# First rows of x ahead of the weights, constant rows behind the first store, a new table of rules

## The chip, the core and the metric

The kernel runs on one core of a Trainium2 chip. The metric is the device time of one execution in microseconds (us), as the median of several runs. Five engines work side by side, each through its own instruction stream in order: TensorE (PE, with its weight loads shown as PEld), VectorE (DVE), ScalarE (ACT), GpSimd (POOL) and SyncE (SP). In this kernel SP issues all the DMAs; "SPq" in a profile is the queue from which it does so.

## What is computed

Eight sequences of 1024 tokens with 256 channels go through one layer of four residual blocks, each behind a layer norm: a retention with its own norm, four heads and a gate; a feed-forward block with a shift by one token; an attention of 16 heads with a bias by relative position; and the same feed-forward block again.

```python
x = L0_attn_a_x                                   # (8, 1024, 256)
x = x + _L0_attn_a_ref(_layernorm(x), ln_w, ln_b, Wq, Wk, Wv, Wg, g_norm_w, Wo)
x = x + _L0_ffn_ref(_layernorm(x), W_r, W_k, W_v, mu_r, mu_k)
x = x + _L0_attn_b_ref(_layernorm(x), wq, bq, wk, bk, wv, bv, wo, bo, rel_bias)
x = x + _L0_ffn_ref(_layernorm(x), W_r, W_k, W_v, mu_r, mu_k)
```

Retention runs through a sequence in chunks with a state S per head: scores of a chunk, masked and decayed, times its values, plus the queries times S; then S is decayed and the chunk's keys times values are added. The attention is a softmax over all 1024 keys of scores plus a bias that depends on the distance of query and key alone, in 32 buckets.

## The kernel before

**A recorded program and a planner.** Nothing is issued while the functions of the kernel run. Each call on `act`, `dve`, `pool`, `sp` or `pe` is recorded as an operation (`Plan.record`) with an estimated cost, the operations it has to come after (`before`, found in `touch` from the parts of tiles that it reads and writes), and the target that `plan.target` had. `Plan.issue` then plays a clock of its own: at each step every free engine takes, among its operations whose inputs are done and whose tiles have a free buffer, the one with the lowest target, the older one of two equals. A DMA is taken to occupy SP for 0.4 us and to be done 2.0 us + bytes / 100 GB/s later, however many others are under way. The order so found is each engine's instruction stream. All instructions are issued from one line (L608, in `emit`), which is why groups in the profile are told apart by tiles.

**Rules and turns.** TensorE's choice has a correction. `RULES` holds sixteen rules: what a change of matmul mode costs, how many PSUM buffers must be free before scores are begun, how many sums to keep in hand, and four offsets by kind of matmul. `TURNS` holds one hexadecimal digit for each 20 us of the planned clock (`STRETCH`), which picks the rule of that time. It is a table of 122 digits.

**Stages.** For each sequence b: `retention(b)`, `ffn_front(b)`, `project_b(b)`, eight `maxima` and `shift` (attention scores p with queries as rows, for their maxima), four `weigh` (scores s with keys as rows, exponentials e, sums acc with the values va) and `back(b)` (output projection bop and the second feed-forward block). Their targets let the retention of the next sequence run beside the attention of this one.

**The head.** The first loads are `cm` (constants), `ln`, then `split(wqk, ...)`: two chunks of Wq and Wk into the tiles xo0 and xo1, cast by ScalarE into a rounded half wqk[0] and by VectorE's subtraction into the rest wqk[1]. `retention(0)` has the target -1.0 and loads its rows itself, in `prepare(c)`: a chunk of 256 tokens into xc, bn_stats on VectorE, the reciprocal roots on GpSimd (a_a, a_y, a_t, and at the end the product a_nb). `turn_chunk` makes z on ScalarE, transposes it on TensorE (ntp), evicts it twice on ScalarE and takes the difference on VectorE: nT, in two halves. Then come qps, vps and gps, the projections; ta and tb, the rotary products on VectorE; tps, qkT, aps, at, ops within the chunk and sps for the state S. In the first sequence `swift(b == 0)` sends to VectorE what GpSimd does later.

**later().** With the target -0.9 it is recorded after retention(0) and goes ahead of what of the retention has a later target: the other weights; hot, rel and ups for the bias (written to ud, read back as hk); bps for the bias of the output; and the constant rows of the stacked queries and keys. The DRAM tiles stk[0] (queries) and stk[1] (keys) hold 64 rows per head, in four blocks of 16: three blocks are written by `project_b` (qk, from TensorE's qkp), the fourth, from ROW_SHIFT on, holds constant rows. For the keys these depend on the head: VectorE multiplies stat by a factor fac, which comes from two small broadcast loads d31 and d0 ("d<-in_b_rel"), into kr, sixteen times, and each kr is stored twice. For the queries they are the same for all heads: two DMAs straight from c_stat in DRAM to stk[0] in DRAM, one for each of the two buffers (i = 0, 1; b % 2 picks one). Each repeats 16 rows of 1024 numbers for 16 heads:

```python
c_stat = ap["c_stat"]
for i in range(2):
    sp.dma_start(
        stk[0][i, ROW_SHIFT // AHD],
        bass.AP(tensor=c_stat.tensor, offset=c_stat.offset, ap=[[0, AH], [T, AHD], [1, T]]),
    )
```

**Who reads them.** `load_pair(b, j)` loads k and q of two heads from stk, all four blocks, for `maxima` and `weigh`. For b = 0 that comes after the four chunks of `project_b(0)`.

## Time and profile before

| | us |
|---|---|
| median of 3 runs (lowest to highest) | 2548.52 (2542.09 to 2551.93) |
| the profiled execution | 2557.27 |
| its span, from first to last instruction | 2555.5 |
| TensorE busy | 2476.2 (97%) |
| VectorE busy | 2107.5 (82%) |
| ScalarE busy | 2069.9 (81%) |
| GpSimd busy | 1589.0 (62%) |

The mean granted clock of TensorE is 0.992. The costliest groups on TensorE are acc (529.5 us), p (460.4) and s (456.7), all of the attention. The chain of work that ended last is TensorE for 79% of the span, VectorE for 8%, DMA for 5%, ScalarE for 3%.

In a timeline, a row has the start, the busy time, engine, line, operation, output<-input with shapes, the count of merged instructions, and in square brackets how long the engine had been idle before it and what it had waited for. A table by stage gives, for each stretch, its length, the busy time of each engine with its count of instructions, then TensorE's granted clock, the share of the DMA engines' time and GB/s.

### The profile page before, as it was taken

The numbers are of one execution on the slowest core, as the hardware profiler recorded it, in microseconds if no ns is written. First come the engines' busy times: TensorE is split into PE (matmuls) and PEld (weight loads), VectorE is DVE, ScalarE is ACT, GpSimd is POOL, SyncE is SP. The second block draws the span as 40 slices with busy tenths as digits, with TensorE's granted clock in tenths as the row PEclk, the third lists the DMA queues.
The fourth block names the chain that finished last, engine by engine and source line by source line (L and its number), as shares of the span: only waits on it lengthen the run. The fifth ranks groups of instructions, "written<-read, shape, count | busy, mean of one in ns | idle before, by whom it ended". The sixth has DMA issues, their size and how long they took to land.

```text
span 2555.5 us, 51508 instructions
## 1 busy us (share of the span) xinstructions
PE 2476.2 (97%) x15814; PEld 1459.8 (57%) x15814; DVE 2107.5 (82%) x6230; ACT 2069.9 (81%) x5334; POOL 1589.0 (62%) x2675
## 2 busy tenths in 40 slices
PE   5999999999999999999999999999999999999997
PEld 3887755555555555555555555555555555554555
DVE  6767998888888888988888788888888888788855
ACT  3565598888989888988888789988898888688883
POOL 2467666666756666666656576666666666666642
PEclk9999999999999999999999999999999999999999
DMA  7136322444344333332324333333233344444322
GB/s 175 42 108 150 81 58 68 130 107 112 85 106 105 84 100 101 110 98 79 92 64 119 97 107 102 94 78 109 68 94 93 102 118 115 124 115 113 93 64 72
DMA packets 252224, 251.17 MB, mean 98 GB/s; under 512 B 89042, under 2 KB 226180, under 8 KB 251924
## 3 DMA queue, kind: packets, MB, share of 16 engines
q1 hardware_dynamic: 251956, 247.89, 36.6%
q8 instruction: 132, 2.16, 0.4%
q14 instruction: 136, 1.11, 0.2%
HBM read 151.32 MB, written 98.59 MB: 98 GB/s over the span
## 4 chain that ended last, share of the span: by engine, by line
PE 79%; DVE 8%; DMA 5%; ACT 3%; POOL 2%; issue 1%; SPq 1%; POOLq 0%; DVEq 0%; ACTq 0%
PE acc L608 16%; PE p L608 10%; PE s L608 10%; PE kps L608 4%; PE wps L608 4%; PE yps L608 4%; PE rps L608 4%; PE qkp L608 3%; PE vps L608 3%; PE qps L608 3%; PE gps L608 3%; PE ops L608 3%; DVE pm L608 3%; ACT e L608 2%; PE bop L608 2%
## 5 line engine op out<-in xcount | busy, mean ns | idle before, releaser
L608 DVE TENSOR_REDUCE pm<-p 128x1 f32<-128x512 f32 (+2 forms) x2048 | 1057.2, 557 | 89.7 <-PE p L608 87.9
L608 ACT ACTIVATE e<-s 128x512 f32<-128x512 f32 (+2 forms) x2048 | 1008.0, 527 | 52.8 <-PE s L608 49.3
L608 POOL TENSOR_TENSOR e<-e,hk 128x512 f32<-128x512 f32 (+1 forms) x558 | 614.0, 1107 | 348.7 <-ACT e L608 326.9
L608 PE MATMUL acc<-e,va 128*17 128x512 f32 x4096 | 529.5, 599 | 3.7 <-ACT e L608 3.4
L608 DVE CUSTOM_DVE_ANT_0 jmax<-p,hk 128x256 bf16<-128x256 f32 (+1 forms) x1152 | 427.0, 371 | 111.8 <-PE p L608 106.6
L608 ACT COPY e<-s 128x256 f32<-128x256 f32 (+1 forms) x1116 | 400.0, 358 | 82.3 <-PE s L608 80.2
L608 PE MATMUL p<-k,q 64*128 64x512 f32 x2048 | 460.4, 438 | 5.0 <-DVE pm L608 2.8
L608 PE MATMUL s<-q,k 64*128 64x512 f32 x2048 | 456.7, 436 | 5.8 <-DVE pm L608 3.2
L608 ACT ACTIVATE e<-e 128x512 f32<-128x512 f32 (+1 forms) x576 | 336.2, 586 | 59.0 <-POOL e L608 56.1
L608 PEld LDWEIGHTS p<-k,q 64*128 64x128 f32 x2048 | 207.5, 185 | 248.4 <-ACT e L608 93.7
L608 PEld LDWEIGHTS s<-q,k 64*128 64x128 f32 x2048 | 206.0, 185 | 204.6 <-issue 69.8
L608 PEld LDWEIGHTS acc<-e,va 128*17 128x17 f32 x4096 | 77.7, 95 | 189.5 <-issue 161.6
L608 PE MATMUL kps<-xk,W_k 128*128 128x256 f32 x512 | 130.8, 399 | 10.7 <-DVE xk L608 9.7
L608 PE MATMUL rps<-W_r,xr 128*128 128x256 f32 x512 | 126.8, 390 | 3.0 <-DVE pm L608 1.8
L608 PE MATMUL yps<-W_v,xk 128*128 128x256 f32 x512 | 127.2, 392 | 1.1 <-DVE pm L608 0.5
L608 PE MATMUL wps<-wo_a,gs 128*128 128x256 f32 x512 | 125.7, 388 | 0.6 <-ACT gs L608 0.5
L608 PEld LDWEIGHTS kps<-xk,W_k 128*128 128x128 f32 x512 | 95.2, 195 | 40.7 <-issue 19.3
L608 PE MATMUL qps<-wqk,nT 128*128 128x512 f32 x384 | 106.8, 413 | 7.0 <-DVE nT L608 6.6
L608 PEld LDWEIGHTS rps<-W_r,xr 128*128 128x128 f32 x512 | 93.4, 191 | 34.5 <-DVE pm L608 5.1
L608 PEld LDWEIGHTS yps<-W_v,xk 128*128 128x128 f32 x512 | 93.6, 192 | 28.7 <-issue 12.0
L608 PEld LDWEIGHTS wps<-wo_a,gs 128*128 128x128 f32 x512 | 92.5, 190 | 26.5 <-issue 4.7
L608 POOL TENSOR_TENSOR ao_y<-ao_a,mhalf 128x4 f32<-128x4 f32 x64 | 65.7, 1026 | 66.5 <-DVE ao_a L608 65.8
(185 smaller groups left out, 4175.3 us busy)
## 6 DMA issues: line engine op xcount, KB each, us to landing
stk<-qk SPq DMA_DIRECT2D x192, 256.0 KB
hk<-ud SPq DMA_DIRECT2D x128, 256.0 KB
q<-stk SPq DMA_DIRECT2D x128, 256.0 KB
k<-stk SPq DMA_DIRECT2D x128, 256.0 KB
od<-o SPq DMA_DIRECT2D x64, 256.0 KB
vd<-vst SPq DMA_DIRECT2D x64, 136.0 KB
va<-vd SPq DMA_DIRECT2D x32, 272.0 KB
xc<-in_x SPq DMA_DIRECT2D x32, 256.0 KB
```

Of the source, the lines that this page charges most:

```text
L608: getattr(real, method)(*[be(a) for a in args], **{k: be(a) for k, a in kw.items()})
```

## The change

It has three parts. The load of the first 256 rows of x is recorded at the top, between `ln` and the split of Wq and Wk, with the target -1.1 of the first loads; `prepare(0)` of the first sequence takes that tile and issues no load. The two loads of the queries' constant rows leave `later()` for a function `constant_rows()`, called once, between `project_b(0)` and the first `maxima`. There they get the target -0.6 and, in the planner, one more operation to come after: the first store of queries (`stored[0]`). The load of stat stays where it was. And TURNS is another table of the same length, whose first three digits are the same.

```diff
 TURNS = (
-    "00070270877472bf8931ef967bfe1d0522ff04383dfe37be3f1f7ef668e19e9c33271224f3e73df5"
-    "5663e6176b19fd77763fbb3cafd79ff9fb9bf84111"
+    "0002022d5122719e9e58f469e3ffb30b577ab1d479fd79649f0576fe7dd0a2e7f1f59d76f22b7b64"
+    "d9edfed755b4febfbed95f00c5b15b912e8bbda111"
 )
...
+    first = plan.tile([P, HALF], F32, "xc", "xc", 4)
+    sp.dma_start(
+        first.rearrange("p (n d) -> p n d", n=2), x[0][:CT, :].rearrange("(n p) d -> p n d", p=P)
+    )
     split(wqk, ("a_Wq", "a_Wk"))
...
-        c_stat = ap["c_stat"]
-        for i in range(2):
-            sp.dma_start(
-                stk[0][i, ROW_SHIFT // AHD],
-                bass.AP(tensor=c_stat.tensor, offset=c_stat.offset, ap=[[0, AH], [T, AHD], [1, T]]),
-            )
         stat = plan.tile([P, T], F32, "k", "stat", NJ)
-        sp.dma_start(stat[:NSTAT], c_stat[1])
+        sp.dma_start(stat[:NSTAT], ap["c_stat"][1])
...
+    stored = []
+
+    def constant_rows():
+
+        c_stat, start = ap["c_stat"], len(plan.ops)
+        plan.target = -0.6
+        for i in range(2):
+            sp.dma_start(
+                stk[0][i, ROW_SHIFT // AHD],
+                bass.AP(tensor=c_stat.tensor, offset=c_stat.offset, ap=[[0, AH], [T, AHD], [1, T]]),
+            )
+        for op in plan.ops[start:]:
+            op.before.add(stored[0])
...
-            t = tile2k("xc", 4).rearrange("p (n d) -> p n d", n=2)
-            sp.dma_start(t, rows_in(x[b], c))
+            t = (first if b == c == 0 else tile2k("xc", 4)).rearrange("p (n d) -> p n d", n=2)
+            if b or c:
+                sp.dma_start(t, rows_in(x[b], c))
...
-                    sp.dma_start(rows_of(s, b, t0, p), pt[i].bitcast(F32))
+                    stored.append(sp.dma_start(rows_of(s, b, t0, p), pt[i].bitcast(F32)).n)
...
         project_b(b)
+        if b == 0:
+            constant_rows()
         for j in range(NPAIR):
```

## The prediction

> **What bounds the kernel now.** I read the page's busy times first, then tables of busy time by stage, then the timeline of the first 60 us, and last the queue that issues the DMAs (SP) around the place where the constant rows are to go.

> ```profile
> PE 2476.2 (97%) x15814; PEld 1459.8 (57%) x15814; DVE 2107.5 (82%) x6230; ACT 2069.9 (81%) x5334; POOL 1589.0 (62%) x2675
> ```

> TensorE is busy 2476.2 of 2555.5 us, so 79.3 us are idle. Where they lie decides what a change of order can win. Tables by stage put 31.2 us of them before 60 us, 14.1 us after 2500 us, and 34 us in the 2440 us between. The fields that matter in the next lines are the stretch, PE's busy time (first), DVE's (third), and near the end the granted clock, the share of the DMA engines and GB/s.

> ```profile
> 0.00:20.40 20.40, 2.91 (x8) 1.08 (x8) 8.19 (x22) 6.97 (x11) 7.74 (x29) 1.00 0.87 280
> 20.40:26.49 6.09, 1.45 (x2) 0.12 (x2) 0.00 (x0) 3.91 (x8) 0.00 (x0) 1.00 0.81 245
> 26.49:51.43 24.94, 15.86 (x88) 12.06 (x89) 21.89 (x46) 8.15 (x19) 2.57 (x3) 0.94 0.76 139
> 60.00:100.00 40.00, 39.52 (x260) 32.77 (x259) 28.69 (x66) 23.59 (x53) 18.05 (x57) 1.00 0.02 8
> ```

> The first 26 us are bound by DMA (0.81 to 0.87 of the engines' time); VectorE does nothing at all for 6.09 us; then VectorE is the bound up to 51.43 (21.89 of 24.94 us); from 60 us on TensorE is. So what the head gains, the end gains: behind it stands a full TensorE. The timeline says why VectorE stood still:

> ```profile
> 3.60 0.43 SPq L608 DMA_DIRECT2D xc<-in_x  x1
> ...
> 9.33 0.75 DVE L608 BATCH_NORM_STATS2 a_st<-xc 128x6 f32<-128x256 f32 x2 [1.33 <-DMA xc<-in_x]
> ...
> 14.84 0.64 SPq L608 DMA_DIRECT2D stk<-in_c_stat  x1
> ...
> 16.83 0.51 SPq L608 DMA_DIRECT2D stk<-in_c_stat  x1
> ...
> 17.36 1.09 ACT L608 ACTIVATE z<-xc,a_nb,a_y 128x256 f32<-128x256 f32 x2
> ...
> 18.47 0.92 SPq L608 DMA_DIRECT2D d<-in_b_rel  x2
> ...
> 26.49 0.16 DVE L608 TENSOR_TENSOR d<-d,d 16x16 f32<-16x16 f32 x1 [6.09 <-DMA d<-in_b_rel]
> ...
> 29.59 0.67 DVE L608 TENSOR_TENSOR nT<-z,nT 128x512 fp32r<-128x512 f32 x1
> ...
> 30.31 2.93 PE L608 MATMUL qps<-wqk,nT 128*128 128x512 f32 x6 [6.56 <-DVE nT L608]
> ...
> 50.54 0.40 DVE L608 COPY S<-sps 128x256 f32<-128x256 f32 x1
> ...
> 51.43 1.23 PE L608 MATMUL ops<-S,qkT 64*128 64x128 f32 x8 [5.25 <-ACT S L608]
> ```

> Two small loads (d, 1 KB each) land 7.5 us after their issue because two loads of constant rows, 16 x 16 x 1024 x 4 bytes = 1 MB each, stand before them. VectorE keeps its order, so nT, whose input ScalarE had finished by 22.4, waits behind d, and the first projection waits for nT. Later TensorE waits 5.25 us for S, which stands in VectorE's queue behind the sixteen kr products. That the constant rows hold the queue up is also in SP's waits:

> ```profile
> SPq L608 <- DMA stk<-in_c_stat: 3.9, 2, 2.7
> ```

> **The change, part by part.**

> (1) *Constant rows out of the head.* SP loses two issues (0.64 + 0.51 us), so the second d load goes out at 18.93 - 1.15 = 17.8. How fast it then lands no row shows, so it is bounded: by the first pair of weights, 3.2 us (second half issued at 2.18, cast at 5.40), and by the load of bwk, 5.4 us (issued 22.41, used 27.79). That is 21.0 or 23.2 instead of 26.49: 5.5 or 3.3 us won, and not above 6.09, the whole wait. I take 5.5: of the some 3.0 MB moved between 15 and 26.5 us (264, 303 and 120 GB/s), 2.1 are the constant rows, so little is left ahead. VectorE's queue itself is at 20.4 then, so the wait falls to some 0.6 us; what is late next is ups, hot and bwk, which arrive on the same queue earlier too.

> (2) *First rows of x ahead of the weights.* The issue moves from 3.60 to the third place, 1.70, past four weight loads (512 KB). It should land about when the first weights now do, 5.4, against 9.33: 3.9 us. That is not what the end gains. Its statistics were through at 14.6 (nb, the last input of z, ends then), yet z ran at 17.36, since ScalarE was held in front of it by the two casts of wg_a (15.49 and 16.84, waiting for their DMA). If the new order leaves z behind them, nothing is won beyond (1). If z goes first, the first projection could start near 17.4 (x at 5.4, the 5.3 us from there to the end of the nb chain as now, ScalarE free of the casts of wv_a at 11.3, then z, transposes, evictions and nT, 6 us as now from 17.36). Even so VectorE is the bound up to 51.43: the resumption of TensorE moves by no more than the work that VectorE can pull into its 12.2 idle us before 20.4: nT 0.67, ta 0.69 + 0.75, tb 0.74, vs 0.69 = 3.5 us. Bounds 0 to 3.5 more; I take 3.5, since the idle time is three times that. The weights passed land 256 KB later, 0.9 us at 282 GB/s; hidden, because the casts (5.40 to 8.0) come long before the first projection; without that cover 0.9 us.

> (3) *Constant rows after the first store.* Both issues stand now on SP behind the first store of queries. No other engine queues behind that store's wait; on SP what follows is:

> ```profile
> 101.28 0.89 SPq L608 DMA_DIRECT2D stk<-qk  x2
> ...
> 106.12 1.45 SPq L608 DMA_DIRECT2D stk<-qk  x3
> 126.83 0.36 SPq L608 DMA_DIRECT2D xd<-xc  x1
> ...
> 194.07 5.61 SPq L608 DMA_DIRECT2D q<-stk  x7
> ```

> Their first reader is q at 194.07. They take up to 8.7 us of the DMA engines (issued 16.83, released SP at 25.5, then beside other loads), and those are at 0.13 between 110 and 120 us. What can suffer is the load of xc at 104.03, read at 112.7: if the rows got ahead of it, 104.03 + 3.2 + 8.7 = 115.9, 3.2 us late. They become due only when the store is through, some microseconds after 101.28, so I take 0, with 0 to +3.2; a gain is excluded, since nothing there waits for less traffic. [...]

> (4) *The table of rules.* Its first three digits are the same, so the first 60 planned us keep their rules; from then on TensorE's choices differ nearly everywhere. No row shows the new order. Estimate from the spread of the present one: TensorE's idle time in the 24 stretches of 100 us from 100 to 2500 has a mean of 1.4 us and a deviation of some 1.25, so a whole order deviates by 1.25 x the root of 24 = 6 us, and the difference of two by 9. I take 0, with -9 to +9.

> Sum: -5.5 - 3.5 + 0 + 0 = **-9.0 us**. The profiled execution took 2557.27 us (span 2555.5 and 1.8 around it), so it would be 2548.3; it lay above the runs shown (2542.09 to 2551.93). On their median: 2548.52 - 9.0 = **2539.5**. The terms' ends give 2548.5 - 18.6 = 2530 and 2548.5 + 8.9 = 2557.

> [...]

> **Rivals.** *A: as summed,* 2539.5, own range 2530 to 2549.

> *B: the new order also loses a stall.* The present one has one bad place:

> ```profile
> 2180.00:2200.00 20.00, 14.70 (x84) 8.13 (x82) 15.53 (x54) 12.07 (x32) 10.85 (x17) 0.97 0.82 194
> 2200.00:2220.00 20.00, 20.00 (x99) 11.63 (x100) 14.45 (x41) 12.17 (x32) 14.43 (x25) 0.86 0.34 101
> ```

> There `bop` waited 4.8 us for `ob`, whose loads stood behind loads of pairs at a DMA share of 0.82, and the clock lost 20 x 0.03 + 20 x 0.14 = 3.4 us more: 8.2 together. It hangs on which loads meet, so another order need not have it: 2539.5 - 8.2 = 2531. Against it: the same chance can place one elsewhere.

> *C: the head doesn't do what it says.* If d stays behind other loads (wg, bwq, stat and hot are still ahead) and z behind the casts, only the 3.3 us of (1) or less remain: about 2546.

> *D: slower.* The new rules bring more stalls of just that kind, loads of the back stage meeting those of the pairs; there are eight such stages and one shows it now. Three more cost 24.6 us against the 9 won: 2564. It makes the kernel slower by over 0.5% from the third on ((12.7 + 9) / 8.2 = 2.6). For it: the planner gives each DMA a fixed latency, so it can't see such a meeting. Against it: seven of eight are free of it now.

> **How the numbers follow.** A measurement of this kernel tells about 0.5% from no change, 12.7 us: faster means below 2535.8, slower above 2561.3. Chances: A 0.44, of which 0.16 lies below 2535.8; B 0.28; C 0.08; D 0.20, of which 0.19 lies above 2561.3. Faster 0.16 + 0.28 = 0.44; same 0.28 + 0.08 + 0.01 = 0.37; slower 0.19. The time is A's, 2539.5. The range runs from 2520, below B's 2531 by the spread of (4), to 2565, which takes in A, C and the nearer half of D; about 0.05 is left below it and 0.10 above.

> **What would show it.** (1) is right if no load from c_stat is issued before 100 us and VectorE's wait for d is under 1.5 us. (2) is right if x's statistics start near 5.4 and the first qps before 22; C if qps starts after 25. TensorE's work after S should resume near 42.4 (51.43 - 9.0); if it resumes at 46 or later, VectorE's kr products or their stores set the head, and (2) was worth nothing. (3) is wrong if VectorE waits for xc between 105 and 130 us. (4): TensorE's idle time between 60 and 2500 us, 34 now; near 25 shows B, above 55 with a clock under 0.95 in several stretches shows D. The prediction fails most likely by (4), whose size nothing here shows.

## The result, and the profile after

| | before | after |
|---|---|---|
| median (lowest to highest), 9 runs each | 2547.17 (2542.09 to 2551.93) | 2557.92 (2556.54 to 2562.86) |
| the profiled execution | 2557.27 | 2556.74 |
| TensorE idle, 0 to 60 us | 31.2 | 25.2 |
| TensorE idle, 100 to 2500 us | 34.1 | 44.1 |
| TensorE busy, whole span | 2476.2 | 2472.1 |

The ratio is 1.0035, with an interval from 1.0026 to 1.0044: 10.8 us slower by the medians, where 9 less were forecast. It is inside the half per cent that I had called "no change", but nine runs of each are enough to tell it from nothing. The two profiled executions do not show it: that of before lay 10 us above its median, that of after 1 us below. So the two profiles are compared place by place, and the size of the change is taken from the timed runs.

First the page's busy times, which hardly moved; "after" does the same work:

```profile
PE 2472.1 (97%) x15814; PEld 1455.5 (57%) x15814; DVE 2109.2 (83%) x6230; ACT 2068.7 (81%) x5334; POOL 1588.0 (62%) x2675
```

The table by stage of after, in the stretches shown of before (length, PE, PEld, DVE, ACT and POOL busy; then granted clock, DMA share, GB/s):

```profile
0.00:20.40 20.40, 2.91 (x8) 1.08 (x8) 7.62 (x28) 6.17 (x10) 7.11 (x29) 1.00 0.75 237
20.40:26.49 6.09, 3.13 (x7) 2.48 (x8) 4.90 (x10) 5.10 (x11) 0.00 (x0) 1.00 0.59 108
26.49:51.43 24.94, 20.22 (x110) 14.93 (x109) 22.72 (x46) 9.91 (x23) 6.70 (x13) 0.87 0.66 139
60.00:100.00 40.00, 39.54 (x267) 33.40 (x266) 27.02 (x62) 23.36 (x54) 15.40 (x46) 1.00 0.10 29
550.00:600.00 50.00, 44.72 (x291) 23.67 (x289) 38.90 (x120) 40.30 (x108) 30.54 (x50) 0.95 0.53 139
2180.00:2200.00 20.00, 19.22 (x107) 10.94 (x99) 17.16 (x52) 13.66 (x36) 12.36 (x21) 1.00 0.88 225
```

VectorE, which stood still from 20.40 to 26.49, is now busy for 4.90 of these 6.09 us, and TensorE has 20.22 instead of 15.86 us of work in the next stretch. The one bad stretch of before, 2180 to 2200, is better (19.22 for 14.70). But 550 to 600 is new: 5.3 us idle, although the DMA share is only 0.53.

The timeline of after's first 60 us, in the lines that answer to those of before:

```profile
1.71 0.43 SPq L608 DMA_DIRECT2D xc<-in_x  x1
5.79 0.43 DVE L608 BATCH_NORM_STATS2 a_st<-xc 128x6 f32<-128x256 f32 x1 [4.12 <-DMA xc<-in_x]
...
13.14 1.09 ACT L608 ACTIVATE z<-xc,a_nb,a_y 128x256 f32<-128x256 f32 x2 [2.24 <-POOL a_nb L608]
...
16.91 0.87 SPq L608 DMA_DIRECT2D d<-in_b_rel  x2
...
17.11 1.86 PE L608 MATMUL bps<-wo_b,bv 128*1 128x256 f32 x4 [17.11 <-DMA bv<-in_b_bv]
...
18.90 1.11 PE L608 MATMUL ntp<-cm,z 128*128 128x128 f32 x4
...
19.34 0.15 DVE L608 TENSOR_TENSOR d<-d,d 16x16 f32<-16x16 f32 x1
...
22.63 0.67 DVE L608 TENSOR_TENSOR nT<-z,nT 128x512 fp32r<-128x512 f32 x1
...
23.36 2.93 PE L608 MATMUL qps<-wqk,nT 128*128 128x512 f32 x6 [3.35 <-DVE nT L608]
...
44.31 0.79 PE L608 MATMUL ops<-S,qkT 64*128 64x128 f32 x8 [3.52 <-ACT S L608]
```

The head does what the change says. VectorE's wait for d (6.09 us) is gone: d starts at 19.34 instead of 26.49. The first projection starts at 23.36 (30.31 before) and the work behind S at 44.31 (51.43): 7 us earlier. And the constant rows leave where they were meant to, with 92 us to go to their first reader:

```profile
101.03 0.87 SPq L608 DMA_DIRECT2D stk<-qk  x2
101.95 1.27 SPq L608 DMA_DIRECT2D stk<-in_c_stat  x2
```

The 7 us are given back later. These are the rows of after's timeline behind the largest idle times of TensorE between 100 and 2500 us; in each of these four, a DMA was late for the engine that releases TensorE, or for TensorE itself:

```profile
595.85 0.55 DVE L608 RECIPROCAL sums<-sums 128x64 f32<-128x64 f32 x1 [5.29 <-DMA sums<-od]
...
597.17 0.79 PE L608 MATMUL s<-q,k 64*128 64x512 f32 x2 [4.55 <-DVE pm L608]
...
941.83 0.43 DVE L608 BATCH_NORM_STATS2 a_st<-xc 128x6 f32<-128x256 f32 x1 [4.40 <-DMA xc<-in_x]
...
943.08 0.47 PE L608 MATMUL s<-q,k 64*128 64x512 f32 x1 [1.81 <-DVE pm L608]
...
2262.28 1.26 POOL L608 TENSOR_TENSOR ob<-ob,os 128x512 f32<-128x512 f32 x1 [7.70 <-DMA ob<-od]
...
2263.59 3.68 PE L608 MATMUL bop<-wo_b,ob 128*128 128x256 f32 x8 [3.55 <-POOL ob L608]
...
2324.40 0.74 PE L608 MATMUL s<-q,k 64*128 64x512 f32 x2 [2.15 <-DMA q<-md]
```

The first pair of lines reads: VectorE had the reciprocal of the sums next in its order, and their load, issued at 593.64, released it 2.2 us later; the pm that would have freed a PSUM buffer stood behind it, and TensorE had nothing to do for 4.55 us. With a fifth one (p at 201.95, 2.43 us, for which the profile names no wait, and 0.39 for a load of k behind it) these stalls are 14.9 us. Before had one of this size:

```profile
2199.95 3.78 PE L608 MATMUL bop<-wo_b,ob 128*128 128x256 f32 x8 [4.79 <-POOL ob L608]
```

The difference is as large as the 10.0 us by which TensorE's idle time in the middle grew. That it fits so well is partly chance: waits of 1.0 to 1.6 us are 10.0 us in before (eight of them) and 3.8 us in after (three), and the waits under 1 us make up for that.

### The profile page after: what moved, and what is told of

Same layout as the page of the kernel before. It is cut to its first block, busy times and chain, and to the rows that moved or that the text cites. A ratio compares the mean times of both kernels' runs of the same rounds, so it can differ in the third digit from the quotient of the medians.

```text
span 2554.7 us, 51543 instructions
## 1 busy us (share of the span) xinstructions
PE 2472.1 (97%) x15814; PEld 1455.5 (57%) x15814; DVE 2109.2 (83%) x6230; ACT 2068.7 (81%) x5334; POOL 1588.0 (62%) x2675
## 3 DMA queue, kind: packets, MB, share of 16 engines
q8 instruction: 133, 2.18, 0.4%
## 4 chain that ended last, share of the span: by engine, by line
PE 77%; DVE 11%; DMA 5%; ACT 4%; POOL 2%; issue 1%; SPq 0%; POOLq 0%; DVEq 0%; ACTq 0%
PE acc L608 15%; PE p L608 10%; PE s L608 10%; PE kps L608 4%; PE wps L608 4%; DVE pm L608 4%; PE yps L608 4%; PE rps L608 4%; PE qkp L608 3%; PE qps L608 3%; PE ops L608 3%; PE gps L608 3%; PE vps L608 3%; ACT e L608 2%; DVE xr L608 2%; PE bvp L608 2%
## 5 line engine op out<-in xcount | busy, mean ns | idle before, releaser
L608 DVE TENSOR_REDUCE pm<-p 128x1 f32<-128x512 f32 (+2 forms) x2048 | 1057.3, 557 | 82.9 <-PE p L608 81.0
L608 ACT ACTIVATE e<-s 128x512 f32<-128x512 f32 (+2 forms) x2048 | 1006.6, 528 | 51.9 <-PE s L608 47.4
L608 POOL TENSOR_TENSOR e<-e,hk 128x512 f32<-128x512 f32 (+1 forms) x558 | 611.9, 1104 | 318.1 <-ACT e L608 304.1
L608 DVE CUSTOM_DVE_ANT_0 jmax<-p,hk 128x256 bf16<-128x256 f32 (+1 forms) x1152 | 427.9, 371 | 133.3 <-PE p L608 127.8
L608 PE MATMUL acc<-e,va 128*17 128x512 f32 x4096 | 526.6, 599 | 1.0 <-ACT e L608 0.6
L608 ACT COPY e<-s 128x256 f32<-128x256 f32 (+1 forms) x1116 | 400.1, 358 | 92.9 <-PE s L608 90.4
L608 PE MATMUL p<-k,q 64*128 64x512 f32 x2048 | 460.9, 438 | 6.5 <-DVE pm L608 2.5
L608 PE MATMUL s<-q,k 64*128 64x512 f32 x2048 | 452.2, 435 | 13.2 <-DVE pm L608 10.3
L608 ACT ACTIVATE e<-e 128x512 f32<-128x512 f32 (+1 forms) x576 | 335.3, 587 | 39.2 <-POOL e L608 36.1
L608 PEld LDWEIGHTS p<-k,q 64*128 64x128 f32 x2048 | 207.6, 185 | 243.1 <-ACT e L608 75.8
L608 PEld LDWEIGHTS s<-q,k 64*128 64x128 f32 x2048 | 203.3, 185 | 197.2 <-issue 73.0
L608 PEld LDWEIGHTS acc<-e,va 128*17 128x17 f32 x4096 | 79.0, 96 | 197.4 <-issue 168.9
L608 PE MATMUL rps<-W_r,xr 128*128 128x256 f32 x512 | 127.5, 391 | 8.7 <-DVE xr L608 5.2
L608 PE MATMUL kps<-xk,W_k 128*128 128x256 f32 x512 | 129.0, 395 | 4.8 <-DVE xk L608 3.8
L608 PE MATMUL yps<-W_v,xk 128*128 128x256 f32 x512 | 127.2, 392 | 1.0 <-POOL xk L608 0.6
L608 PE MATMUL wps<-wo_a,gs 128*128 128x256 f32 x512 | 125.5, 388 | 1.2 <-DVE pm L608 0.5
L608 POOL TENSOR_TENSOR ao_y<-ao_a,mhalf 128x4 f32<-128x4 f32 x64 | 66.0, 1031 | 81.9 <-DVE ao_a L608 81.1
L608 PEld LDWEIGHTS rps<-W_r,xr 128*128 128x128 f32 x512 | 93.0, 191 | 38.3 <-issue 6.2
L608 PEld LDWEIGHTS kps<-xk,W_k 128*128 128x128 f32 x512 | 94.3, 193 | 33.2 <-issue 12.3
L608 PE MATMUL qps<-wqk,nT 128*128 128x512 f32 x384 | 108.3, 418 | 3.9 <-DVE nT L608 3.3
L608 PEld LDWEIGHTS yps<-W_v,xk 128*128 128x128 f32 x512 | 93.8, 192 | 29.2 <-issue 11.8
L608 PE MATMUL vps<-wv_a,nT 128*128 128x512 f32 x384 | 106.0, 412 | 0.9 <-DVE pm L608 0.8
```

The lines of the kernel that those rows point to most:

```text
L608: getattr(real, method)(*[be(a) for a in args], **{k: be(a) for k, a in kw.items()})
```

## The experiments

**Each part with a table that was not found for it.** The first four kernels put the parts together anew: (e1) after with the old table, (e2) before with the new table, (e3) before with the load of x first, and (e4) before with the constant rows late. e1, e3 and e4 have the old table.

```diff
# e1: head of the change, old TURNS        # e2: old head, new TURNS
+    first = plan.tile([P, HALF], F32, "xc", "xc", 4)          # e1, e3
+    sp.dma_start(first.rearrange(...), x[0][:CT, :].rearrange(...))
...
+    def constant_rows():                                      # e1, e4
...
-    "00070270877472bf8931ef967bfe1d0522ff04383dfe37be3f1f7ef668e19e9c33271224f3e73df5"
+    "0002022d5122719e9e58f469e3ffb30b577ab1d479fd79649f0576fe7dd0a2e7f1f59d76f22b7b64"   # e2
```

> The change without its table: first rows ahead, constant rows late, the old digits. Head as in the changed kernel: first qps near 23.4 us, work after S resumed near 44.3, 7.1 us before the old kernel. Theory T (the new digits' order costs the 17 us that lie between the head's -7 and the +10.75 measured): 2547 - 7 = 2540. Theory R (the late constant rows cost it): 2557 as with the new digits. Theory L (every change of order is a draw, because DMAs land later than the planner thinks wherever they meet; the old kernel's draw was a good one): the head moves everything against the digits' stretches, so this is a new draw too, anywhere in 2535 to 2562, with other stalls at other places than either kernel, each behind a late DMA.

> The old kernel with the new digits alone: head as before (qps near 30.3, resumed near 51.4). Theory T: 2547 + 17 = 2564. Theory R: 2547, the digits cost nothing. Theory L: a new draw with the head's 7 us not won, 2542 to 2569, with stalls at places that are not those of the changed kernel, so that the two parts do not add.

> The old kernel with the first rows ahead of the weights alone; constant rows early, old digits. By my sum the head gains little here: VectorE still waits for d behind the constant rows, so first qps 28 to 30 us and work after S resumed 49 to 51.4. Theory T: 2545 to 2547. Theory R: 2545 to 2547. Theory L: 2540 to 2565, a new draw.

> The old kernel with the constant rows late alone; x behind the weights, old digits. By my sum the wait for d falls from 6.09 to about 0.6 us, first qps near 25 and work after S resumed near 46. Theory T: 2547 - 5.5 = 2541.5. Theory R: 2553 or more. Theory L: 2536 to 2562, a new draw.

| | ratio to before [interval] | first qps | work behind S | TensorE busy | idle 100 to 2500 |
|---|---|---|---|---|---|
| before, profiled | 1 | 30.31 | 51.43 | 2476.2 | 34.1 |
| e1, head, old table | 1.0188 [1.0156, 1.0221] | 23.34 | 44.39 | 2511.9 | 41.1 |
| e2, new table, old head | 1.0406 [1.0374, 1.0439] | 28.32 | 48.28 | 2526.5 | 69.9 |
| e3, x first, old table | 1.0340 [1.0315, 1.0366] | 27.95 | 49.40 | 2530.6 | 57.1 |
| e4, rows late, old table | 1.0240 [1.0214, 1.0266] | 24.37 | 44.07 | 2509.7 | 58.8 |

All four are 51 to 104 us slower than before, by the medians, far beyond any term of mine. The heads themselves are fine (e1's is that of after, e4's resumes at 44.07); the loss is behind them. More of it is busy than idle time: TensorE is busy 34 to 54 us longer for the same 15,814 matmuls. The costliest groups of e2 show two thirds of its 50 us (group, count, then busy us and mean ns of one; first e2, then before):

```profile
L608 PE MATMUL acc<-e,va 128*17 128x512 f32 x4096 | 535.0, 600 | 2.5 <-ACT e L608 1.6 <-ACT o L608 0.8
L608 PE MATMUL p<-k,q 64*128 64x512 f32 x2048 | 479.1, 444 | 18.8 <-DVE pm L608 7.6 <-issue 2.7 <-DVE xo L608 2.5
L608 PE MATMUL s<-q,k 64*128 64x512 f32 x2048 | 465.7, 439 | 9.1 <-DVE pm L608 6.7 <-ACT e L608 0.5 <-DVE ao_a L608 0.2
...
L608 PE MATMUL acc<-e,va 128*17 128x512 f32 x4096 | 529.5, 599 | 3.7 <-ACT e L608 3.4
L608 PE MATMUL p<-k,q 64*128 64x512 f32 x2048 | 460.4, 438 | 5.0 <-DVE pm L608 2.8
L608 PE MATMUL s<-q,k 64*128 64x512 f32 x2048 | 456.7, 436 | 5.8 <-DVE pm L608 3.2
```

One p takes 444 ns, but 2048 of them are 909 us and the group is busy for 479: nearly two run at a time. Before has 460.4 us of p at 438 ns. A single matmul is thus nearly as long as it was, and fewer of them overlap. The three groups together are busy for 1479.8 us in e2 and 1446.6 before, which is 33 of the 50 us.

Why, the kernel's planner tells when it is run alone, without a chip: its own clock ends at 2423.1 us for before and 2427.1 for after, but at 2493.2, 2519.3, 2521.4 and 2497.7 for e1 to e4. With 200 random tables of digits it ends at 2541 on average, whichever the head. And one digit changed among the first twenty of before's table makes it 2495 on average, one among the digits 100 to 119 only 2436. So a table is not a set of good rules for certain times; it is one exact path, and anything that shifts the plan early throws the rest back more than halfway to a random one (72 of 118 us on average). The parts of this change can't be valued by swapping them under a fixed table: these four runs answer another question than the one I had put.

**Other tables for either head.** The next four have the same heads, each with a table searched anew for that head: e5 and e6 the new head, e7 and e8 the old.

> The changed kernel with yet another table, searched for its own order; the planner's own clock ends at 2424.3 (the old kernel's at 2423.1, the changed one's at 2427.1). Head as in the changed kernel (first qps 23.4, resumed 44.3). Theory F (a table fits one order; between two fitted tables the chip's time differs by the planned clocks and by how many DMAs land later than planned; the head's 7 us do reach the end): device time less planned clock is 124 for the old kernel and 131 for the changed one, an unlucky one; here some 117 to 124, so 2541 to 2548. Theory R (the late constant rows or the early x cost time further on, whatever the table): 2424.3 + 131 = 2555 again.

> The same head with a third table, planned clock 2424.5. Theory F: 2541 to 2549, and the distance to the run before shows how far two fitted tables of one planned clock lie apart (I think up to 8 us). Theory R: 2555.

> The old kernel with another table, searched for its own order; planned clock 2422.7. Head as before (first qps 28 to 30, resumed 48 to 51). Theory F: the old kernel's offset of 124 with the spread of tables, so 2542 to 2555, and on the mean of two tables 5 to 7 us over the new head. Theory R: 2547, and 5 to 10 us under the new head.

> The old kernel with a third table, planned clock 2427.4, as good a plan as the changed kernel's. Theory F: 2427.4 + 124 = 2551, within 2546 to 2560. Theory R: 2551, with the new head's runs at 2555.

| | planner's clock | ratio to before [interval] | TensorE busy | idle 100 to 2500 |
|---|---|---|---|---|
| e5, new head | 2424.3 | 1.0070 [1.0049, 1.0092] | 2477.5 | 47.9 |
| e6, new head | 2424.5 | 1.0004 [0.9992, 1.0016] | 2472.8 | 36.1 |
| e7, old head | 2422.7 | 1.0065 [1.0044, 1.0085] | 2477.7 | 43.6 |
| e8, old head | 2427.4 | 1.0011 [0.9999, 1.0023] | 2471.8 | 36.3 |

Two tables whose plans end within 0.2 us of each other (e5, e6) are 17.6 us apart on the chip by their medians (2569.39 and 2551.76), where I had thought of up to 8; of the four ranges that I had given for these runs, only that of e8 holds. In the profiles, 11.7 us of it are idle time in the middle and 4.7 busy time. The lottery of the table is larger than what the head can win, and both heads have drawn good and bad ones.

**The same order, with only the loads moved.** To value the head, the order must not be drawn again. So e9 to e11 let the planner make its order and change it afterwards, on SP's queue alone: e9 is the order of before with the two loads of constant rows moved behind the fifth store of qk; e10 also moves the load of x ahead of the weights; e11 is the order of after with the two loads moved back ahead of stat. e12 is before once more.

```diff
-                    self.emit(op, [t for t, _, _ in got])
+                    self.order.append((op, [t for t, _, _ in got]))
...
+    def finish(self):
+        for what, where, shift in self.moves:
+            item = self.order.pop([op.n for op, _ in self.order].index(what))
+            self.order.insert([op.n for op, _ in self.order].index(where) + shift, item)
+        for op, news in self.order:
+            self.emit(op, news)
...
+    plan.moves = [(rows[1], stored[4], 1), (rows[0], stored[4], 1)]
```

> The old kernel with every engine's order kept as the old planner made it; only the two loads of constant rows are taken out of SP's stream after the planning and put behind the first chunk's fifth store of qk (near 102 us). Nothing else moves. If the head's gain reaches the end (theory F): VectorE's wait for d below 1.5 us instead of 6.1, first qps near 24 to 25, work after S resumed 44 to 46, and 6 us off the end: ratio 0.9975, about 2542 where the old kernel has 2548. If it is swallowed by later waits of the same order: head as said and ratio 1.000. Theory R (the late rows cost time where they are): ratio above 1.001.

> The run before it, with the load of the first rows of x also moved, to stand before the first weights on SP. VectorE's order still has nT behind d, two kr and the copy of ups, so I expect nothing beyond the rows: within 1 us of the run before it (ratio 0.9975). My prediction's term (2) would give another 3.5 us: ratio 0.996.

> The changed kernel with every engine's order kept, and only the two loads of constant rows put back into the head, before the load of stat. If the head's gain reaches the end: VectorE waits for d again (5 to 7 us), work after S resumed near 50, and 6 us over the changed kernel: 2564, ratio to the old kernel 1.006 where the changed kernel has 1.0035. Theory R: they cost more late than early, so at or under 2558, ratio 1.002 to 1.0035.

> The old kernel itself, for a second profile: ratio 1.000, within 0.002. Its profiled execution took 2557, above the median of its runs by 9 us. If a typical execution does not have the stall at 2194 to 2200 us (4.8 us idle and a lower clock after it), this profile has TensorE idle some 5 us less between 2100 and 2200 us and a span near 2547.

| | ratio to before [interval] | first qps | work behind S | idle 0 to 60 | idle 100 to 2500 |
|---|---|---|---|---|---|
| e9, old order, rows late | 0.9962 [0.9948, 0.9976] | 23.99 | 44.63 | 25.2 | 35.7 |
| e10, old order, rows late, x first | 0.9974 [0.9963, 0.9984] | 23.96 | 44.56 | 25.6 | 33.6 |
| e11, new order, rows early | 1.0060 [1.0045, 1.0076] | 29.90 | 51.68 | 31.3 | 48.1 |
| e12, before again | 1.0006 [0.9995, 1.0016] | 31.08 | 51.98 | 32.6 | 33.7 |

This settles the first two terms. Two lines of e9's timeline, the end of VectorE's wait and the first projection:

```profile
20.18 0.16 DVE L608 TENSOR_TENSOR d<-d,d 16x16 f32<-16x16 f32 x1
...
23.99 2.69 PE L608 MATMUL qps<-wqk,nT 128*128 128x512 f32 x6 [2.67 <-DVE nT L608]
```

and two of e11's, where only those loads are back in the head:

```profile
25.87 0.16 DVE L608 TENSOR_TENSOR d<-d,d 16x16 f32<-16x16 f32 x1 [7.12 <-DMA d<-in_b_rel]
...
29.90 2.92 PE L608 MATMUL qps<-wqk,nT 128*128 128x512 f32 x6 [10.55 <-DVE nT L608]
```

Moving two DMAs and nothing else brings 6.8 us in the head (S at 44.63 instead of 51.43) and takes 7.4 (51.68 instead of 44.31), and the end follows: e9 is 9.4 us faster than before by the medians (2543.29 against 2552.65; by the interval 6 to 13), and after is 0.25% (6.4 us) below e11. Loading x first on top of it (e10 against e9) changes neither qps nor S, and not the end (0.9974 against 0.9962, the intervals overlap).

It also gives the price of the new order. e11 has the old place of the rows, and x first, which was worth nothing in the old order; what is left is the order, and it is 0.60% slower (15 us, interval 11 to 19). Its profile and that of e12, from the same series, show what kind of time it is (e11 first):

```profile
100.00:2500.00 2400.00, 2351.94 (x15183) 1362.83 (x15182) 2006.64 (x5995) 2004.47 (x5198) 1533.50 (x2514) 1.00 0.36 98
...
100.00:2500.00 2400.00, 2366.31 (x15252) 1372.72 (x15254) 2010.61 (x6019) 2014.11 (x5217) 1542.61 (x2530) 1.00 0.37 98
```

TensorE is idle for 14.4 us more in this stretch, while its busy time over the whole span is nearly the same (2472.9 and 2474.2 us). The five stalls of after are all there again in e11, with 2.81, 5.12, 1.82, 3.97 and 2.77 us; e12 has the one of before, with 5.22. The matmuls overlap no less: the three groups of the attention are busy for 1440.4 us in e11 and 1439.7 in after, and for 1442.6 to 1447.1 in the five profiles of the old order (before, e9, e10, e12 and e14 below). So the price of this order is idle time.

e12 was to tell whether the stall of before at 2180 to 2200 is an accident of one execution. I expected it to be smaller; it is there again, in full:

```profile
2180.00:2200.00 20.00, 14.28 (x73) 8.84 (x70) 12.94 (x47) 10.10 (x27) 10.87 (x19) 0.89 0.81 195
```

So it belongs to the order, as after's stalls do, which e11 repeats.

**One stall taken away, and plans with slower DMAs.** e13 is the order of after with each reciprocal of the sums, and its store, put up to six VectorE operations later, so that VectorE does not stand before a load that is still under way; e14 is e9 with the same. In e15 the planner counts 3.0 us + bytes / 60 GB/s for a DMA instead of 2.0 us + bytes / 100 GB/s, with a table found for that; e16 is the new head with one more table found as before.

```diff
+        for pair in self.later:
+            at = {op.n: i for i, (op, _) in enumerate(self.order)}
+            end = min(at[a.n] for n in pair for a in self.ops[n].after if a.n not in pair)
+            start = at[pair[0]]
+            after = [i for i in range(start + 1, end) if self.order[i][0].eng == "DVE"][:6]
...
-                op.cost, op.tail = 0.4, 2.0 + size / 100000.0
+                op.cost, op.tail = 0.4, 3.0 + size / 60000.0
```

> The changed kernel, all orders kept but for the sixteen reciprocals of sums and their stores, which go up to six VectorE operations later. Theory W (single waits for late DMAs make the idle time): VectorE's waits for sums<-od (9.6 us in five, longest 5.3) fall below 4, the stall of 4.6 us at 594 falls to under 2, and the time falls by 3 to 6 us: ratio 1.0011 to 1.0023 where the changed kernel has 1.0035. Theory S (the stalls only show where slack is taken up; the order's whole sum of waits costs): the waits fall, the time stays, 1.003 to 1.004.

> The old order with the constant rows late, and the reciprocals later in the same way. That order has 6.6 us of waits for sums but no stall of TensorE behind them. Theory W: no change within 2 us, ratio 0.9955 to 0.9970. Theory S: a gain of up to 3 us.

> The changed head; the planner takes a DMA to be done 3.0 us + bytes / 60 GB/s after its issue instead of 2.0 us + bytes / 100 GB/s, and the table is searched for that; its planned clock is 2425.2. If the planner's optimism about DMAs makes the difference between device time and planned clock (124 to 145 us for tables fitted so far), it shrinks: TensorE's idle time between 100 and 2500 us at or under 34 us, ratio 0.994 to 0.999. If not: an ordinary fitted table, ratio 0.9995 to 1.007, idle 36 to 48.

> The changed kernel with a fourth table, planned clock 2418.7 (the changed kernel's 2427.1, the old one's 2423.1). If planned clock and head both count and the rest is the tables' spread: 2418.7 + 126 to 145 = 2545 to 2564, ratio 0.998 to 1.005, most likely 1.000.

| | ratio to before [interval] | median | TensorE busy | idle 100 to 2500 |
|---|---|---|---|---|
| e13, new order, sums late | 1.0028 [1.0019, 1.0037] | 2556.00 | 2473.8 | 40.9 |
| e14, old order, rows and sums late | 0.9984 [0.9973, 0.9995] | 2545.61 | 2472.3 | 33.6 |
| e15, new head, slow DMAs planned | 0.9962 [0.9949, 0.9974] | 2539.81 | 2464.9 | 38.0 |
| e16, new head, another table | 0.9954 [0.9942, 0.9967] | 2539.14 | 2465.5 | 39.2 |

In e13 the stall behind the sums is gone. The stretch that had 44.72 us of TensorE in after:

```profile
550.00:600.00 50.00, 48.55 (x315) 26.00 (x315) 42.08 (x129) 44.67 (x119) 33.11 (x52) 1.00 0.53 139
```

That is 3.8 us of work more, at the same DMA share. VectorE's waits for the sums fall from 9.6 to 2.0 us and TensorE's idle time in the middle by 3.2 us, the ratio from 1.0035 to 1.0028, some 2 us where the theory of single waits had 3 to 6; the intervals overlap, so this is a hint and no proof that the late DMAs are what the new order costs. In the old order the same edit takes these waits from 6.6 to 0.3 us and wins nothing (e14, 0.9984, against e9, 0.9962, where I had expected 0.9955 to 0.9970).

e16 (its plan ends at 2418.7) and e15 beat both kernels: 10.6 and 9.9 us below before, which had 2549.71 beside them; for e16 I had expected a ratio of 0.998 to 1.005. They have the head of the change, and e16's is in time what after's is (S at 44.55; 43.58 in e15). e16's groups show where the time went:

```profile
L608 PE MATMUL acc<-e,va 128*17 128x512 f32 x4096 | 525.2, 597 | 5.3 <-ACT e L608 5.0 <-ACT o L608 0.3
L608 PE MATMUL p<-k,q 64*128 64x512 f32 x2048 | 456.6, 439 | 3.6 <-DVE pm L608 1.9 <-DVE xc L608 0.9 <-DVE xo L608 0.4
L608 PE MATMUL s<-q,k 64*128 64x512 f32 x2048 | 450.6, 436 | 7.5 <-DMA q<-md 4.9 <-DVE pm L608 1.3 <-DVE xo L608 0.7
```

Together 1432.4 us, 14.2 less than before's 1446.6 and 10 less than in any profile of the old order, with single matmuls about as long as ever: more of them overlap. Its idle time in the middle is no better than before's (39.2 against 34.1). So an order has two prices, how much its matmuls overlap and how often it meets a late DMA, and the table moves both. e15 doesn't tell the planner's DMA times from the luck of a table: e16, with the old times, does as well, and the idle time of at most 34 us that I had named as the sign did not come (38.0).

## Why the prediction was wrong, by its own steps

**(1) Constant rows out of the head, -5.5 (bounds 3.3 to 6.1): the mechanism was right, its size a little small.** The wait for d went from 6.09 us to nothing, not to some 0.6, since d landed before VectorE came to it (20.18 in e9, 19.34 in after). No load of the constant rows is issued before 100 us, as the sign for it asked (the load of stat, from c_stat too, stays at 14.73). The head won 6.8 us in e9, which is above the whole wait that I had set as a bound, and the end 9.4 there (6 to 13) and 6.4 in the new order, by the ratios of after and e11.

**(2) x first, -3.5 (bounds 0 to 3.5): worth nothing, the lower bound.** x's statistics started at 5.79, and z did go ahead of the casts of wg_a, at 13.14. But I had counted the way from z to the first projection as 6 us "as now", and followed it on ScalarE and VectorE only. In TensorE's order the transposes ntp stand behind bps, which waits until 17.11 for the load of bv, so they began at 18.90. From there nT, behind d, fac and the first three kr on VectorE, came at 22.63. The condition I wrote down ("the first qps before 22") was missed by 1.4 us, and S at 44.31 lies between my 42.4 and the 46 at which the term was to be worth nothing. e9 and e10 show that it was worth nothing even so: S comes at 44.63 without x first and at 44.56 with it. They have the old order; in the new one no run leaves x first out, but there S comes at 44.31, no more than 0.3 us earlier than in e9.

**(3) The rows late, 0: right.** VectorE doesn't wait for xc between 105 and 130 us in after, and e9 with the rows at 100.81 loses nothing. Left in the head they cost 6 to 13 us by e9: behind them on SP stood the loads d, for which VectorE waited 6.09 us in before.

**(4) The table, 0 with -9 to +9: this is the step that failed.** It was mis-sized: 15 us (11 to 19) instead of 0. Two things were wrong in it. The spread came from the idle time of one order in its 24 stretches, as if stretches were drawn afresh; but orders differ in busy time too (2464.9 to 2477.7 us among those with fitted tables, 2469.5 to 2476.2 among five profiles of the old one), which that estimate leaves out, and e5 and e6 are 17.6 us apart. And the middle, 0, took the old order for an average one. Of five fitted tables with the new head, two are 10 us better than before, one equal, and two worse, among them the changed kernel's; the two others with the old head are 2 and 14 us above it. With what the head is worth by e9 and e11 (0.25 to 0.38%) put back on those with the new head, the six other orders lie 7 to 9 us above the old one on average, and the best of them, e16, 2 to 5 below. That is an estimate from few tables, but it says that the old table was a good draw: a new one was to be expected some 8 us above it, and this one came out at 15.

With the sizes as measured, the sum is -6.4 for (1), 0 for (2) and (3), and +15.3 for (4), together +8.9, which is the ratio of 1.0035. That they meet is no further proof: e11 stands between before and after, so its two distances have to add up. By way of e9, the other run that stands between them, they are -9.7 and +18.6. The forecast was 18.4 us below the median measured; (4) is most of that, and (2) is 3.5. One reading was a little off, and nothing hangs on it: of before's idle time, 13.6 us lie after 2500 us and 34.6 between 60 and 2500, where the forecast had 14.1 and 34.

**The rivals.** B was half right: the stall at 2180 to 2200 is gone with the new order. D's mechanism came to pass, more stalls behind late DMAs, four and an unnamed one against one, but not all where I had put it (one of the five waits for `ob` in a back stage; three others wait for the sums, for x and for a load of q, and for the fifth the profile names no wait) and not at its price: 44.6 us of idle time between 60 and 2500 us where I asked for more than 55 to call it D, and a granted clock that was 1.00 over that stretch. The forecast named (4) as the step it would most likely fail by, and gave D 0.20. Of the five tables with the new head one (e5) is slower by more than 0.5%, so that chance was not too small; what was wrong is the middle of (4).

**What stays open.** That the new order costs 15 us is shown with the order held, and e11's profile has nearly all of it as idle time of TensorE (14.4 us). What makes this idle time is shown in part: four of after's five large stalls stand behind a late DMA (12.1 us), and the removal of one of them brought some 2 us, which the intervals don't tell from nothing. The others were not removed.

## What to carry to other kernels

An order that a search has fitted to one program is part of the measurement: swap an early instruction and the fit is gone (51 to 104 us here), search again and the chip deals another hand (up to 18 us at equal planned time). So value an edit with the order held, by moving its instructions after planning, and time several fitted orders before one is kept. And follow a moved input down every engine's order to the consumer that matters: x came 3.5 us earlier and stood still behind a bias that was waiting for its own load.

## What the hardware showed that was not expected

**Two loads of 1 KB waited with two of 1 MB ahead of them on the same queue.** The loads d were issued at 16.91 in after and used at 19.34, with no wait; in before they were issued at 18.47 and waited for until 26.49, with the two loads of constant rows ahead of them. e9 differs from before, and e11 from after, in the place of those two loads alone, and there the wait goes and comes back (7.12 us in e11). No run sends them over different queues, so whether their place in the queue or the load of the DMA engines (0.81 of their time from 20.40 to 26.49 in before) held the small loads back is not told apart.
